# A block's finer steps on another table of openings, and its leftovers run at the block's close

## The chip, the core and the metric

One program runs on one core of a Trainium2 chip. The metric is the device time in microseconds (us). The engines are TensorE (PE in the profile), VectorE (DVE), ScalarE (ACT), GpSimd (POOL) and the queue of SyncE (SP), which only issues DMAs here.

## The reference, cut to what matters

`x` has 16 graphs of 1024 nodes with 128 features, and all share one sparse adjacency matrix (about 8 edges a node). Four layers follow one another: attention, graph attention, attention, attention.

```python
# attention layer (L0, L2, L3): 8 heads of 16
Q, K, V = h @ Wq, h @ Wk, h @ Wv
scores = einsum('bnhd,bmhd->bhnm', Q, K) / sqrt(16)          # -inf where adj == 0
attn_out = einsum('bhnm,bmhd->bnhd', softmax(scores), V)
x = layer_norm(h + attn_out @ Wo + bo, ln1)
x = layer_norm(x + relu(x @ W1 + b1) @ W2 + b2, ln2)
# graph attention layer (L1): one head
h = x @ W
e = leaky_relu(h @ a_src + (h @ a_dst).T, 0.2)                # -inf where adj == 0
x = layer_norm(softmax(e) @ h + x)
```

## The kernel before, in words

The kernel works on the edges alone. Nodes are sorted by degree into eight tiles of 128 (t = 0 to 7); the 16 graphs form two groups of eight (g = 0, 1), and a group two halves of four. A unit is a layer, a group and a tile, (l, g, t); there are 64 of them, in this order. I call the stretch in which the edges of one unit are worked on its block.

A block has parts: pairs of gathered slots, and one part with a single mixed slot, which is always part 3. Tile 0 has six parts, tiles 1 to 6 have five, tile 7 has four. So the block of tile 0 is the long one, that of tile 7 the short one. In an attention layer DVE does three operations on every part i, at 2.3 us each (1.2 us for the mixed one): the product of gathered keys and queries (`products`, L963), the reduction to scores (L986), and, one part later, the weighting of the gathered values with the exponentials (`weighted`, L1014). The exponential is made by ACT (L990). The keys and values come by indirect DMA, issued by POOL (L951) four parts ahead into one of four buffers; a buffer is free again after the weighting. The products have four buffers of their own. PE gives one back when `summed` (L1030, `acc<-pr,marks`) has added a part up. Parts 0 and 1 are added up together, at the start of the third iteration.

When all parts of a unit are added up, PE sums the denominators (`divided`, L1030 `ps<-ex,marks`), and DVE divides (L1067, L1070). The division stands in DVE's queue behind the first weighting of the next block. What follows is the unit's tail: output projection, two layer norms, the hidden layer, and the projection to the next layer's table. It runs on PE and ACT, beside the next block. There are two tails, a for half 0 and b for half 1. Each is a generator with these steps:

- 1: transposes of o on PE (L647), copy on ACT (L653). 2: bias, ACT (L716). 3: Wo and centring, PE (L720, L721).
- 4: squares, ACT (L624). 5: Ln and Exp, ACT (L630, L631). 6: scaling, ACT (L640).
- 7: transposes of z on PE (L647), gain and shift on ACT (L655). 8 and 9: the two halves of W1 on PE (L731) with the ReLU on ACT (L740).
- 10 and 11: W2 and centring, PE (L745, L749). 12 to 14: as 4 to 6. 15: transposes and gain for the new state (L647, L655); from here on the tail counts as free.
- 16 and 17: projection to the next layer (PE L576, ACT L580; to the graph layer L596). 18: the table is written by SP. In the last layer 16 transposes back, and 18 writes the output by POOL; there no tail ever counts as free, so it always runs to its end.

A third kind of generator stands in the list `fronts`: the queries of the next unit (`queries`). Its steps for half 0 are: Wq on PE (L904) and a copy to q (L908); four replications on PE (L913) and two copies to qr (L916); the other two copies. The same three follow for half 1; the seventh call finds it at its end. In the first group of layer 0 the list also holds `slots`, which makes index tiles: PE spreads (L413) and DVE unpacks (L427). After the fronts come `loads` (state of a later unit; in layer 0 with transposes of x, L647) and `slow` (the first projection of the second group, in layer 0 alone).

The order is written out by hand: the engines work through their queues as the program puts the instructions there. Between DVE's operations the main loop calls `others()`, which I call an opening. After the division of an attention unit the openings are counted from 0, and each takes one string from the table `PLAN`: "a" and "b" run one step of tail a or b, "q" one step of the fronts. The openings fall as follows in a block of five parts, D being the division:

- entry 0 follows D. 1, 2, 3 follow product 2, its reduction, and the weighting of part 1.
- 4, 5, 6 follow product 3 (mixed), its reduction, and the weighting of part 2. The sum of parts 0 and 1 is put into PE's queue just ahead of entry 4.
- 7, 8, 9 follow product 4, its reduction, and the weighting of part 3.
- 10, 11, 12 follow product 0 of the next block, its reduction, and the weighting of part 4. 13 and 14 follow product 1 of that block and its reduction; the denominators are put ahead of 13. Then comes the next D.

So a block of five parts has 15 openings, that of six 18 and that of four 12. Past the end of the table an opening runs "abq". Where an attention unit is to be closed and a tail isn't yet free, the loop in lines 1243 to 1247 runs further openings until both are. What a tail has not done by then it does in the next block, ahead of the new tail of its half, since `planned` steps the first generator it finds.

Of the kernel before, what the change touches and what calls it, by code (L numbers as in the profile page):

```python
# [137 lines left out]
def sparse_path(ctx: ExitStack, tc: tile.TileContext, a: dict, out: bass.AP, flag):  # L138
# [64 lines left out]
    def gather_buffer():  # L203
        return gathers.tile([P, max(4 * ROW, J * (ROW + G))], F32, tag="e", name="e")
# [605 lines left out]
    def at_once(g):  # L810

        spare = reps.tile([P, J, ROW], F32, tag="qr", name="spare")

        def fetch(t):
            if t < T:
                nc.sync.dma_start(
                    spare[:, t % J, :], a["x"][t * P : (t + 1) * P, columns(g, 0, HF)]
                )

        for t in range(3):  # L820
            fetch(t)
        yield
        for t in range(T):
            fetch(t + 3)
            rows = spare[:, t % J, :].rearrange("p (h g d) -> p h g d", h=HF, g=GH)
            both = []
            for h in range(HF):
                kv = None
                if h:
                    kv = (hidden, queries_of_shared)[t % 2]()  # L830
                    kv = kv.rearrange("p (c g d) -> p c g d", c=2, d=D)
                both.append(natural(g, t, h, rows[:, h], kv))
            while both:
                advance(both)
                yield

    PLAN = (
        "qaaqqbaba", "", "aq", "abb", "a", "qaba", "abbqabba", "", "baqbaba", "qqb", "bqaa", "", "b", "qbqqqbq", "ba",
    )

    def exponents():
# [14 lines left out]
    def is_attention(u):  # L856
        return LAYERS[units[u][0]][1] is ATTN
# [101 lines left out]
    def products(i):  # L959
        u, (piece,) = parts[i]  # L960
        n = len(piece)
        prs[i] = [prods.tile([P, 2, ROW], F32, tag="pr", name="pr")]
        nc.vector.tensor_tensor(  # L963
            prs[i][0][:, :n, :], es[i][:, :n, :ROW],
            qx[u].rearrange("p (o c) -> p o c", o=1) if (MIX, 0) in piece
            else of_piece(qs[u], piece),
            ALU.mult,
        )
# [132 lines left out]
    opening = [None]  # L1101
    half_of = {}

    def step(gen, gens):
        got = next(gen, "end")
        if got == "end":
            gens.remove(gen)
        elif got == "free":
            free.append(gen)

    def planned(beyond="abq"):
        n = opening[0]
        opening[0] += 1
        for c in PLAN[n] if n < len(PLAN) else beyond:
            if c == "q":
                aside()
                continue
            for gen in tails:
                if half_of[gen] == "ab".index(c):
                    step(gen, tails)  # L1120
                    break
# [18 lines left out]
    def aside():  # L1140
        while True:
            gens = fronts or loads or idle()
            if not gens:
                break
            got = next(gens[0], "end")
            if got == "end":
                gens.pop(0)
                continue
            if got == "idle":
                advance(idle())  # L1150
            break
# [3 lines left out]
    with tc.manual_schedule():  # L1155
        wide = [gather_buffer() for _ in range(EDGES)]
        setup, entry, weights = graph(wide), at_once(0), load_weights("L0")
        next(setup)
        next(weights)
        next(entry)  # L1160
        more = [weights, load_graph_weights()]
        rest = slots()
        for i, room in enumerate(setup):
            if i == T:
                for gen in more:
                    next(gen)
            if room == "load":
                for _ in loaded(0):
                    next(entry, None)
            elif room == "queries":  # L1170
                for _ in entry:
                    pass
                for _ in queries(0):
                    pass
            elif isinstance(room, str):
                next(rest)
            else:
                for _ in range(room):
                    next(entry, None)
        for _ in entry:  # L1180
            pass
        scratch.close()
        prods = ctx.enter_context(tc.tile_pool(name="prods", bufs=4))
        smalls = ctx.enter_context(tc.tile_pool(name="smalls", bufs=3))
        slow.append(at_leisure(1))
        second = loaded(1)
        next(second)
        for i in range(AHEAD - 1):
            gathered(i)
        nc.gpsimd.memset(wide[3], 0.0)  # L1190
        gathered(AHEAD - 1)
        fronts.extend([islice(rest, 4), second] + more)
        closing, sizes = None, ()
        begun = 0
        for i in range(len(parts) + 2):
            here = i < len(parts)
            u = parts[i][0] if here else len(units)
            if here:
                l = units[u][0]
                eager[0] = 1 if u < 2 else 0  # L1200
                if i and parts[i - 1][0] != u:
                    begun = i
                    if u < T - 1:
                        fronts.append(islice(rest, 4))
                    if l + 1 < len(LAYERS) and LAYERS[l + 1][1] is ATTN:
                        if units[u][1:] == (0, 1):
                            more = load_weights(LAYERS[l + 1][0])
                            next(more)
                            next(more)
                        if units[u][1:] == (0, 4):  # L1210
                            fronts.append(more)
                if is_attention(u):
                    products(i)
            if i > 1:
                summed(i - 2)
                done = parts[i - 2][0]
                if parts[i - 1 : i] == [] or parts[i - 1][0] != done:
                    closing = divided(done)
                    next(closing)
            others()  # L1220
            if here:
                exponentials(i)
            if here and i == begun + 1:
                if is_attention(u):
                    shared(u)
                while loads:
                    advance(loads)
                if u + 1 < len(units):
                    fronts.append(queries(u + 1))
                loads.append(loaded(u + 2))  # L1230
                if u:
                    advance(loads)
            others()
            if 0 < i <= len(parts):
                weighted(i - 1, 0)
                if not is_attention(parts[i - 1][0]):
                    others()
                    weighted(i - 1, 2)
                gathered(i - 1 + AHEAD)
                for _ in sizes:  # L1240
                    pass
            if closing is not None and here:
                while any(gen not in free for gen in tails):
                    if opening[0] is None:
                        advance(tails)
                    else:
                        planned("ab")
                next(closing)
                sizes, closing = closing, None
                passes = 3 if is_attention(u) else 4  # L1250
                steps = STEPS if is_attention(done) else GRAPH_STEPS
                steps -= LATE[units[done][0]]
                pace[:] = 0.0, steps / (passes * sum(part[0] == u for part in parts) - 1)
                if is_attention(done) and opening[0] is None:
                    for gen in list(tails):
                        if gen in free:
                            for _ in gen:
                                pass
                            tails.remove(gen)
                opening[0] = 0 if is_attention(done) else None  # L1260
            others()
            if i + 1 >= len(parts) or parts[i + 1][0] != u:

                while fronts:
                    advance(fronts)
        while opening[0] < len(PLAN):
            planned()
        while tails:
            advance(tails)
        for _ in closing:  # L1270
            pass
        while tails:
            advance(tails)
# [435 lines left out]
```

## Time and profile before

| | |
|---|---|
| median of 3 runs | 2240.71 us (2234.82 to 2246.4) |
| the profiled execution | 2224.11 us |
| its span on the core | 2222.3 us, clock granted to TensorE 0.958 on the mean |
| steady blocks (tiles 1 to 6), division to division | 33 to 36 us; in layer 0, group 0, about 42.8 us |
| blocks around a short one, e.g. from 1289.3 us | 32.8 us (short), then 45.1 us (long) |

A row of the groups or of a timeline gives the line, the engine, the operation and the tiles (out<-in); in a timeline the start and the duration come first, and brackets at the end hold the idle time of the engine before the row and what ended it. A line of the waits says which engine and line waited for which, how long in total, how often, and the longest.

### The profile page before, as it was taken

The page shows a single profiled execution, that of the slowest core. Times are in us where ns is not written, and L with a number is a line of the kernel's source. Part 1 is how long each engine was busy: PE and PEld are TensorE (multiplying, and loading weights), DVE is VectorE, ACT ScalarE, POOL GpSimd, SP SyncE. Part 2 cuts the span into 40 slices and gives each one's busy share as a digit, 9 for nine tenths or more (in the row PEclk, how much of TensorE's full clock was granted, in tenths as well). Part 3 has the DMA queues.
Part 4 walks back from the last instruction along what each step waited for, and adds up shares of the span by engine and source line. Part 5 has one row for each costly group of instructions (what it writes and reads, how often), then busy time and mean ns, then how long its engine had stood idle before and what let it go on. Part 6 is the DMA issues. An engine that isn't in the chain of part 4 may idle for free.

```text
span 2222.3 us, 36516 instructions
## 1 busy us (share of the span) xinstructions
PE 2009.0 (90%) x13140; PEld 1265.3 (57%) x13140; DVE 1874.3 (84%) x1472; ACT 1520.1 (68%) x5041; POOL 1029.4 (46%) x699
## 2 busy tenths in 40 slices
PE   7589998989999889989899998999989899989986
PEld 5446665655665555555466665656655555555654
DVE  7887888889998477767999988999888988899892
ACT  3337776868887555556587886888767777677774
POOL 3342433444455477774444535355343444454540
PEclk8799999999999999999999999999999999999998
DMA  7888777768988699998888987899878788678850
GB/s 257 292 298 279 285 248 269 281 235 298 323 318 295 209 332 354 351 348 320 319 320 323 330 292 277 314 335 326 291 270 303 272 284 283 224 278 298 285 210 21
DMA packets 164701, 636.05 MB, mean 286 GB/s; under 512 B 34569, under 2 KB 37385, under 8 KB 116015
## 3 DMA queue, kind: packets, MB, share of 16 engines
q0 software_dynamic: 88720, 485.08, 61.1%
q1 hardware_dynamic: 75792, 148.57, 19.4%
q8 instruction: 105, 1.72, 0.3%
q14 instruction: 84, 0.68, 0.1%
HBM read 581.08 MB, written 92.34 MB: 303 GB/s over the span
## 4 chain that ended last, share of the span: by engine, by line
PE 57%; DVE 14%; ACT 12%; issue 9%; DMA 5%; POOL 3%; POOLq 0%; DVEq 0%; ACTq 0%
PE acc L1030 14%; PE ps L647 6%; PE ps L913 6%; PE yps L745 6%; PE ps L576 5%; PE ps L731 5%; DMA e<-table,idx 4%; DVE pr L1014 4%; PE yps L721 3%; PE yps L720 3%; DVE pr L963 3%; PE yps L749 3%; DVE sc L986 2%; ACT f L740 2%; POOL e L951 2%
## 5 line engine op out<-in xcount | busy, mean ns | idle before, releaser
L951 POOL DMA_INDIRECT e<-table,idx x576 | 882.2, 1532 | 1017.7 <-DVE pr L1014 750.9
L1014 DVE TENSOR_TENSOR pr<-e,ex 128x2048 f32<-128x2048 f32 (+1 forms) x320 | 661.5, 2076 | 59.5 <-ACT ex L990 31.9
L963 DVE TENSOR_TENSOR pr<-e,qr 128x2048 f32<-128x2048 f32 x192 | 443.4, 2309 | 116.4 <-ACT qr L916 71.3
L1030 PE MATMUL acc<-pr,marks 128*32 128x512 f32 x2624 | 506.5, 608 | 30.7 <-DVE o L1070 19.1
L986 DVE TENSOR_REDUCE sc<-pr 128x128 f32<-128x2048 f32 (+1 forms) x240 | 497.5, 2073 | 8.0
L624 ACT ACTIVATE z<-yps,root 128x128 f32<-128x128 f32 x888 | 315.4, 377 | 71.3 <-PE yps L749 36.2
L745 PE MATMUL yps<-W,f 128*128 128x128 f32 x1520 | 253.2, 284 | 19.1 <-ACT f L740 19.1
L1030 PEld LDWEIGHTS acc<-pr,marks 128*32 128x32 f32 x2624 | 107.6, 110 | 285.0 <-issue 230.8
L745 PEld LDWEIGHTS yps<-W,f 128*128 128x128 f32 x1520 | 203.2, 191 | 99.4 <-ACT f L740 61.1
L640 ACT ACTIVATE z<-yps,rstd 128x128 f32<-128x128 f32 x888 | 253.8, 373 | 3.0
L916 ACT COPY qr<-ps 128x512 f32<-128x512 f32 x384 | 202.4, 595 | 30.4 <-PE ps L913 24.2
L580 ACT COPY kv<-ps 128x512 f32<-128x512 f32 x176 | 103.3, 593 | 173.2 <-PE ps L576 162.6
L576 PE MATMUL ps<-Wkv,xT 128*128 128x256 f32 x768 | 205.2, 409 | 15.2 <-ACT xT L653 13.1
L731 PE MATMUL ps<-x,W 128*128 128x512 f32 x384 | 187.5, 611 | 15.7 <-ACT x L655 15.7
L913 PE MATMUL ps<-q,rep 32*128 32x512 f32 x768 | 186.4, 688 | 13.4 <-ACT q L908 11.9
L624 ACT ACTIVATION_READ_ACCUMULATOR z<-yps,root 128x1 f32 x888 | 191.7, 216 | 0.0
L576 PEld LDWEIGHTS ps<-Wkv,xT 128*128 128x128 f32 x768 | 144.9, 201 | 69.0 <-ACT xT L653 16.8
L740 ACT ACTIVATE f<-ps,b 128x512 f32<-128x512 f32 x190 | 129.9, 684 | 77.9 <-PE ps L731 77.3
L647 PE MATMUL ps<-ident,z 128*128 128x128 f32 x896 | 152.4, 286 | 14.0 <-ACT z L640 10.9
L721 PE MATMUL yps<-centre,x 128*128 128x128 f32 x768 | 158.4, 290 | 2.7 <-ACT x L716 2.3
L720 PE MATMUL yps<-Wo,oT 128*128 128x128 f32 x768 | 159.6, 292 | 0.6 <-ACT oT L653 0.4
L647 PEld LDWEIGHTS ps<-ident,z 128*128 128x128 f32 x896 | 106.1, 141 | 77.0 <-ACT z L640 49.6
(176 smaller groups left out, 2594.8 us busy)
## 6 DMA issues: line engine op xcount, KB each, us to landing
table<-kv SPq DMA_DIRECT2D x88, 512.0 KB, 7.1
kept<-xT SPq DMA_DIRECT2D x96, 256.0 KB, 5.3
x<-kept SPq DMA_DIRECT2D x48, 512.0 KB, 9.0
qx<-qr SPq DMA_DIRECT2D x48, 256.0 KB, 7.3
e<-table,idx POOLq DMA_INDIRECT x576, 8.0
table<-kv SPq DMA_DIRECT2D x32, 256.0 KB, 8.6
qx<-qr SPq DMA_DIRECT2D x18, 384.0 KB, 6.5
qx<-qr SPq DMA_DIRECT2D x42, 128.0 KB, 5.2
```

The lines of the kernel that those rows point to most:

```text
L576: nc.tensor.matmul(ps[:, k, :], x[:, i + k, :], w[LAYERS[l][0], "Wkv"], start=True, stop=True,)
L624: nc.scalar.activation(z[:, i, :], y[:, i, :], AF.Square, scale=D**-0.5, bias=root, accum_out=total[:, i : i + 1],)
L640: nc.scalar.activation(z[:, i, :], y[:, i, :], AF.Copy, scale=rstd[:, i : i + 1])
L647: nc.tensor.transpose(ps[:, i, :], z[:, i, :], ident)
L731: nc.tensor.matmul(ps, p["W1"][:, f * P : (f + 1) * P], x1.rearrange("p g n -> p (g n)"), start=True, stop=True,)
L745: nc.tensor.matmul(ps[:, i, :], f1[:, f, i * P : (i + 1) * P], p["W2"][:, f, :], start=(f == 0), stop=False,)
L913: nc.tensor.matmul(ps, rep_of(j), q[32 * j : 32 * j + 32], start=True, stop=True)
L951: nc.gpsimd.indirect_dma_start(out=es[i][:, k, :], out_offset=None, in_=tables[l, g][:, :], in_offset=bass.IndirectOffsetOnAxis(ap=idx[:, ...
L963: nc.vector.tensor_tensor(prs[i][0][:, :n, :], es[i][:, :n, :ROW], qx[u].rearrange("p (o c) -> p o c", o=1) if (MIX, 0) in piece else of_p ...
L986: nc.vector.tensor_reduce(sc[:, :n, :], prs[i][0][:, :n, :].rearrange("p k (a d) -> p k a d", d=HD), mybir.AxisListType.X, ALU.add,)
L1014: nc.vector.tensor_tensor(prs[i][k0 // 2][:, :m, :].rearrange("p k (a d) -> p k a d", d=d), es[i][:, k0 : k0 + m, base : base + ROW].rearr ...
L1030: nc.tensor.matmul(outs[32 * j : 32 * j + 32], marks[:, mark, :], rhss, start=(chunk == mine[0]), stop=(chunk == mine[-1]),)
```

## The change

The table `PLAN` holds the same numbers of steps (18 a, 18 b, 15 q over its 15 entries) in other places. And where a unit is closed, all entries of the table that are left are run, after both tails are free and ahead of the division.

```diff
     PLAN = (
-        "qaaqqbaba", "", "aq", "abb", "a", "qaba", "abbqabba", "", "baqbaba", "qqb", "bqaa", "", "b", "qbqqqbq", "ba",
+        "qaaqqba", "baqba", "aq", "a", "bbaa", "abq", "baqbbaa", "", "aqbbba", "", "bbqaa", "b", "", "qqqqbbqq", "ba",
     )
...
                         advance(tails)
                     else:
                         planned("ab")
+                while opening[0] is not None and opening[0] < len(PLAN):
+                    planned()
                 next(closing)
```

By the step numbers above, counted through the two tables, the steps stand in these entries (steps that stay are left out; the calls of q are counted from the queries' first in entry 0):

| step | before | after |
|---|---|---|
| b2, a4 | 0 | 1 |
| a5, query 4 (Wq of half 1) | 2 | 1 |
| b3 | 3 | 1 |
| a6 | 3 | 2 |
| query 5 (replications of half 1, two copies) | 5 | 2 |
| a7 | 4 | 3 |
| b4 | 3 | 4 |
| b5, a8, a9 | 5 | 4 |
| a10, b6 and query 6 (the last two copies) | 6 | 5 |
| a13 | 8 | 6 |
| b13 | 9 | 10 |
| b15 | 12 | 11 |
| query 7 (their end) | 8 | 6 |
| the two calls of q after it | 9, 9 | 8, 13 |

In PE's queue of a steady block two groups change places: the four L913 of half 1 and tail a's four L647 `ps<-ident,z` stood behind the eight L1030 that add up parts 0 and 1, and now stand ahead of them. In layer 0, group 0, four L647 `ps<-ident,x` move from ahead of the spread L413 to behind the denominators. On ACT the last two copies to qr stood behind tail b's L655 and now stand ahead of it. In the short blocks' successors the queries, b's projection and step 18 of both tails come ahead of the new tails' first transposes.

## The prediction

> **What bounds the kernel now.** I read the page's busy times, then single blocks by stretch, the waits, then timelines of single blocks. No engine is full over the span, and none can be named from these shares alone.
>
> ```profile
> PE 2009.0 (90%) x13140; PEld 1265.3 (57%) x13140; DVE 1874.3 (84%) x1472; ACT 1520.1 (68%) x5041; POOL 1029.4 (46%) x699
> ```
>
> The busy time by stretch, for single blocks (columns: length, then busy us of PE, PE's weight loads, DVE, ACT and POOL, clock, DMA share, GB/s), shows where the limit is. The first row is a block of layer 0, group 0; the second one of layer 0, group 1; then a short block, the long one after it, and two neighbours of layer 3.
>
> ```profile
> 298.60:341.30 42.70, 38.77 (x248) 25.88 (x248) 35.70 (x39) 29.70 (x101) 16.11 (x11) 0.92 0.74 261
> 566.20:599.60 33.40, 32.55 (x230) 20.84 (x229) 32.42 (x19) 27.96 (x99) 16.95 (x11) 1.00 0.92 330
> ...
> 1289.30:1322.10 32.80, 31.76 (x216) 21.30 (x214) 25.48 (x17) 27.64 (x88) 11.11 (x8) 1.00 0.79 278
> 1322.10:1367.20 45.10, 39.58 (x229) 22.39 (x230) 39.16 (x23) 28.38 (x89) 20.22 (x13) 1.00 0.77 264
> 1978.40:2013.60 35.20, 33.28 (x213) 20.44 (x214) 32.19 (x19) 25.76 (x85) 17.34 (x11) 0.90 0.85 304
> 2013.60:2048.60 35.00, 32.25 (x220) 19.68 (x218) 32.38 (x19) 27.09 (x88) 18.93 (x12) 1.00 0.80 292
> ```
>
> A steady block holds 32.3 us of DVE work and lasts 33 to 36 us: DVE sets the pace, PE is nearly as full, and only what makes DVE wait can be won. So the waits of DVE, by line (total, times, longest):
>
> ```profile
> DVE pr L963 <- ACT qr L916: 71.3, 22, 8.4
> ...
> DVE pr L1014 <- ACT ex L990: 31.9, 19, 5.3
> ...
> DVE pr L963 <- DMA e<-table,idx: 28.7, 23, 2.6
> ...
> DVE little L427 <- PE ps L413: 16.2, 5, 3.4
> DVE pr L963 <- PE acc L1030: 8.5, 10, 3.7
> ```
>
> The largest is the first product of a block (product 0), waiting for the last copy of its queries: 22 times, it starts just as that copy ends. The timeline of DVE in the block whose division is at D = 1978.40 shows this and a second, hidden limit.
>
> ```profile
> 1978.40 0.55 DVE L1067 RECIPROCAL both<-ps 128x64 f32<-128x64 f32 x1
> ...
> 1991.77 2.32 DVE L963 TENSOR_TENSOR pr<-e,qr 128x2048 f32<-128x2048 f32 x1
> ...
> 2000.20 2.29 DVE L963 TENSOR_TENSOR pr<-e,qr 128x2048 f32<-128x2048 f32 x1 [2.65 <-ACT qr L916]
> ```
>
> PE between the same times:
>
> ```profile
> 1989.81 1.92 PE L1030 MATMUL acc<-pr,marks 128*32 128x512 f32 x16
> 1991.67 0.66 PE L647 MATMUL ps<-ident,z 128*128 128x128 f32 x4
> 1992.25 2.06 PE L913 MATMUL ps<-q,rep 32*128 32x512 f32 x8
> 1994.24 1.98 PE L731 MATMUL ps<-x,W 128*128 128x512 f32 x4
> ```
>
> The product at 1991.77 (product 4) takes the buffer that this sum (L1030, ahead of entry 4) gives back. It starts 0.04 us after the sum ends: in this block it is late by 0.1 us already. Call the sum's end S, counted from D. Over the blocks S is 13.4 to 14.0 in layer 0 group 0 and where layer 3 was throttled, 11.1 to 11.3 in layer 0 group 1, 10.8 to 11.9 in layer 2; product 4 could start at 13.2. So the sum has 1.3 to 2.4 us to spare in unthrottled blocks and none in the others.
>
> **What the Trainium skill says.** "PSUM — Partial Sum Buffer", section "Engine vs sequencer instructions": ScalarE and VectorE queues are strictly first in, first out, and matmuls run in program order. The trace agrees: the transposes and the queries' matmuls follow the sum without a gap, in the program's order. So whatever is put ahead of the sum delays it by its full length. "TensorE: Matmul & The Clock Gate", section "What's actually happening": half clock after an idle window of some 3.4 us. The trace agrees roughly: idle of 2.85 to 3.8 us before the first transposes after D is followed by 6.8 us at clock 0.5 in five blocks of layer 0 and every other one of layer 3; idle of 1.67 us (at 1321.9) was not.
>
> **The change part by part.** DVE's order, POOL's and its gathers stay; steps on PE and ACT move, and with them their SP writes (table L585 and L610, state L568, 5 to 9 us to landing). Those I cost at nothing: the gathers that read them belong to the next layer, a whole group of eight blocks later.
>
> *1. Queries and step a7 move ahead of the sum.* Old: the four replications of half 1 (L913) in entry 5, a's transposes (step 7) in entry 4, both after the sum. New: entries 2 and 3, both ahead of it. From the second timeline their length is 1992.25 − 1991.67 = 0.58 plus 1994.24 − 1992.25 = 1.99 = 2.58 us. Their inputs are there in time (the q copy moves up behind the squares), so the sum ends at S + 2.58, and product 4 starts at S + 2.62 where that is over 13.2. From product 4 to product 0 DVE needs 5.99 us (13.14 to 19.13 in layer 0 group 1, without a wait): product 0 not before S + 8.61.
> In return the last query copies no longer stand behind b's step 7: on ACT they follow the two ReLUs and the scaling. From the L731 matmuls to the second ReLU's end 2.76, the exponential 0.2, scaling 1.05, copies to release 0.6: queries at S + 2.5 + 4.6 = S + 7.1. Old: S + 8.46 (13.33 + 8.46 = 21.79 = 2000.20 − 1978.40; 11.09 + 8.46 = 19.55, seen 19.55).
> So in a steady block the old wait for queries is taken over by a wait for the sum: S + 8.46 becomes S + 8.61. In 18 steady blocks bound by queries that is 18 × 0.15 = **+2.7 us**. In the others product 0 waits for its gather, whose issue hangs on a weighting ahead of product 4: a gain or loss of nothing, covered by that transfer.
>
> *2. Short blocks* (tile 7: four parts, product 0 of the next block comes right after entry 6; waits 6.5, 7.1, 7.1, 6.0 us). Here no product 4 lies between, so the queries at S + 7.1 instead of S + 8.46 count: 4 × 1.36 = **−5.4 us**.
>
> *3. Layer 0, group 0.* A transposition of x (L647, 0.55 us) moves from entry 9 past the spread (L413), for which DVE waits 3.4 us in five blocks: 5 × 0.55 = **−2.8 us**.
>
> *4. Entries left over.* After a short block in layers 0 and 2 (and at 2→3), the old code leaves b three steps and a one step behind; the long block then ends with waits of 4.33 + 2.31, 4.92 + 0.71 and as much again: 17.9 us. The new loop runs b's projection (steps 16, 17) and the queries at once, ahead of the first transposes. The trace shows this only in layer 3, where the old loop already ran all (division at 1897.7): 5.28 us wait at L1014, at half clock. At full clock I count on ACT, ahead of o's transposes, 2.05 + 0.5 + 1.2 + 2.05 of copies, then to the exponential: it ends at D + 13.3 instead of 10.9, 2.3 us late, and the sum costs another 1.3: 3.65 per block. Ends: 3 × 3.65 − 17.9 = −6.9; with half clock 3 × 6.95 − 17.9 = +3. I take **−5**.
> *5.* Layer 3's own long block: +0.5 (exponential behind step 5; the sum +1.7, of which a later 1.17 wait is saved). Blocks after long ones: waits of 0.8 to 1.2 us from the lag shrink, 3 × −0.5. The first block of layers 0 and 2 loses 0.6 each. Together **+0.2**. Graph layer: only leftovers move, nothing.
>
> Sum: 2.7 − 5.4 − 2.8 − 5 + 0.2 = −10.3 us on the profiled execution's own 2224.11 us (span 2222.3 and 1.8 around it). The median of the runs shown, 2240.71, is 16.6 above that execution; the same share, −0.46%, gives 2230.4, rounded to **2230**.
>
> **Rivals.**
> *R1, the clock recovers.* PE idle before D is 2.85 us in group 0; with the 0.55 us moved into it and DVE earlier by 0.4 it is 1.9. If half clock then stays away in five blocks and in some of layer 3, S falls by 2.6 and product 0 with it: up to 10 × 2.5 more, 2205 to 2225. Against it: idle of 2.1 (at 383.6) still throttled.
> *R2, the boundary pays nothing.* The three long blocks behave like layer 3's: 8 us of my gain go, 2238, no change.
> *R3, slower: the sum's wait comes on top.* Product 4 is late by 2.58 less the slack, 0.2 to 1.3 us in some 40 unthrottled or gather-bound blocks. If the weighting behind it, and so the gathers that it releases, then come late by as much, and each lost time is not given back at product 0, a block loses 0.5 to 1.2: +20 to +48 on my 2230, that is 2250 to 2278. It decides from 0.5 us per block (0.26 eats my gain). For it: the two DMA queues together are busy 80% of the span. Against: the weighting that frees product 0's buffer lies ahead of product 4.
> *R4, nothing but a permutation:* in layer 3 the new loop has nothing to run; then only part 1 to 3 count, 2235.
>
> **How the numbers follow.** A measurement here can tell about 0.5% (11 us) from no change. Forecast 0.50 (half of it over 0.5%), R1 0.16, R2 and R4 0.18, R3 0.16 (0.02 of it within 0.5%). Faster 0.25 + 0.16 = 0.41; slower 0.14; same 0.25 + 0.18 + 0.02 = 0.45. The range leaves out the farther half of R1 and of R3: 2208 to 2256; the forecast's own is 2222 to 2238.
>
> **What would show it.** L963 ← ACT qr falls from 71 to some 25 us (short blocks and the layer starts are left); L963 ← PE acc rises from 8.5 to over 25. In steady blocks S is 2.5 later, product 0 within 0.3 us of its old place. In short blocks the wait is 4.7 to 5.8. Long blocks wait early (D + 13), not at D + 35. A block length of layer 2 changed by over 0.5 us, or another clock pattern, would make this wrong.

## The result, and the profile after

| | before | after |
|---|---|---|
| median, 19 runs each in turn | 2231.42 us | 2219.80 us |
| ratio of after to before | | 0.9939, 95% interval 0.9917 to 0.9962 |
| the profiled execution | 2224.11 us | 2221.51 us |
| its span and mean clock | 2222.3 us, 0.958 | 2219.3 us, 0.955 |

The change gains 0.61%; 0.46% was forecast. The time named, 2230 us, was that share taken off the three runs shown, whose median was 2240.71; 19 runs put the kernel before at 2231.42, and 2219.80 lies 2 us below the forecast's own 2222 to 2238. So it is the share that was met. The busy times of the page hardly move, as an exchange of places should have it:

```profile
PE 1993.9 (90%) x13140; PEld 1260.8 (57%) x13140; DVE 1873.2 (84%) x1472; ACT 1525.9 (69%) x5041; POOL 1028.0 (46%) x699
```

Busy time by stretch, for single blocks of after (columns as in the prediction): layer 0 group 0, layer 0 group 1, a short block, the long one after it, two neighbours of layer 3.

```profile
299.90:341.65 41.75, 37.29 (x248) 25.20 (x248) 36.10 (x40) 30.00 (x101) 16.50 (x11) 0.92 0.75 261
565.30:598.20 32.90, 31.82 (x231) 20.68 (x230) 32.45 (x20) 28.16 (x100) 17.85 (x11) 1.00 0.94 336
1290.60:1321.20 30.60, 29.15 (x204) 19.48 (x203) 25.48 (x17) 26.14 (x85) 11.11 (x8) 1.00 0.84 304
1321.20:1367.80 46.60, 43.75 (x245) 24.92 (x244) 39.13 (x23) 31.01 (x94) 18.40 (x13) 1.00 0.74 257
1973.60:2009.60 36.00, 33.52 (x214) 21.24 (x215) 32.23 (x20) 25.94 (x85) 13.78 (x10) 0.87 0.83 293
2009.60:2045.80 36.20, 31.29 (x219) 19.29 (x217) 32.26 (x19) 27.19 (x88) 16.58 (x12) 0.99 0.84 297
```

The short block is 2.2 us shorter than in the prediction's fence, the long one 1.5 us longer, with 4 us more of PE's work in it. Layer 3 still changes between full and reduced clock from block to block. Now the waits of DVE in after:

```profile
DVE pr L1014 <- ACT ex L990: 47.1, 33, 8.4
DVE pr L963 <- PE acc L1030: 40.6, 27, 4.8
...
DVE pr L963 <- DMA e<-table,idx: 22.1, 19, 3.6
DVE pr L963 <- PE ps L647: 18.9, 5, 5.0
...
DVE little L427 <- PE ps L413: 13.1, 5, 3.3
...
DVE pr L963 <- ACT qr L916: 12.1, 2, 6.8
```

The wait for the queries, the largest before with 71.3 us, is down to 12.1. The 18.9 us put down to L647 belong with it: 17.9 of them are the short blocks, where product 0 still starts just as the last copy to qr ends (the record of that copy ends 0.46 us after the product's start, as it did before). In its place stands the wait for the sum, 40.6 us after 8.5. The block with its division at 1973.56 shows the exchange, first on DVE, then on PE:

```profile
1973.56 0.55 DVE L1067 RECIPROCAL both<-ps 128x64 f32<-128x64 f32 x1
...
1990.31 2.29 DVE L963 TENSOR_TENSOR pr<-e,qr 128x2048 f32<-128x2048 f32 x1 [2.15 <-PE acc L1030]
...
1995.97 2.28 DVE L963 TENSOR_TENSOR pr<-e,qr 128x2048 f32<-128x2048 f32 x1
```

```profile
1985.97 1.14 PE L913 MATMUL ps<-q,rep 32*128 32x512 f32 x8
1987.76 0.66 PE L647 MATMUL ps<-ident,z 128*128 128x128 f32 x4 [0.66 <-ACT qr L916]
1988.35 1.92 PE L1030 MATMUL acc<-pr,marks 128*32 128x512 f32 x16
```

Replications and transposes now run ahead of the sum. Product 4 waits 2.15 us for it, at D + 16.7, and product 0 comes at D + 22.4 without a wait. In the prediction's block it came at D + 21.8 with a wait of 2.65.

One profile is not enough for a difference of 14 us, and the first profile of before lay under its median. A second one was taken of each kernel (runs `before_again` and `after_again`). These are the lengths of blocks, from division to division, added up by kind, in us:

| kind (blocks) | before, two profiles | after, two profiles | only the table | only the loop | loop without queries |
|---|---|---|---|---|---|
| layer 0 group 0, its first block | 48.5, 49.1 | 53.8, 52.3 | 52.3 | 49.0 | 52.1 |
| layer 0 group 0, next five | 206.9, 206.9 | 203.7, 201.9 | 201.6 | 205.9 | 198.7 |
| short (4) | 129.3, 128.9 | 120.3, 121.9 | 121.2 | 129.9 | 121.9 |
| long after short (4) | 182.0, 181.9 | 186.5, 184.2 | 186.2 | 183.7 | 173.8 |
| first after a long one (3) | 103.5, 103.4 | 101.3, 101.4 | 103.0 | 101.6 | 101.9 |
| other steady ones of layers 0 (group 1) and 2 (15) | 509.3, 508.6 | 509.4, 506.2 | 507.6 | 512.1 | 505.9 |
| graph layer (16) | 317.2, 318.6 | 318.3, 317.2 | 326.4 | 317.3 | 316.9 |
| steady ones of layer 3 (12) | 425.8, 426.3 | 430.3, 429.6 | 421.8 | 425.1 | 423.4 |

### The profile page after: what moved, and what is told of

Its sections match the earlier page's. It is cut to its first block, busy times and chain, and to the rows that moved or that the text cites. A ratio compares the mean times of both kernels' runs of the same rounds, so it can differ in the third digit from the quotient of the medians.

```text
span 2219.3 us, 36551 instructions
## 1 busy us (share of the span) xinstructions
PE 1993.9 (90%) x13140; PEld 1260.8 (57%) x13140; DVE 1873.2 (84%) x1472; ACT 1525.9 (69%) x5041; POOL 1028.0 (46%) x699
## 4 chain that ended last, share of the span: by engine, by line
PE 58%; DVE 13%; issue 12%; ACT 8%; DMA 5%; POOL 3%; POOLq 0%; DVEq 0%; ACTq 0%
PE acc L1030 14%; PE ps L647 6%; PE ps L731 6%; PE yps L745 6%; PE ps L913 5%; PE ps L576 5%; DMA e<-table,idx 4%; DVE pr L1014 4%; PE yps L721 3%; PE yps L720 3%; POOL e L951 3%; PE yps L749 3%; DVE pr L963 3%; PE ps L904 2%; DVE sc L986 2%
## 5 line engine op out<-in xcount | busy, mean ns | idle before, releaser
L1014 DVE TENSOR_TENSOR pr<-e,ex 128x2048 f32<-128x2048 f32 (+1 forms) x320 | 661.6, 2076 | 76.1 <-ACT ex L990 47.1
L1030 PE MATMUL acc<-pr,marks 128*32 128x512 f32 x2624 | 505.8, 608 | 27.7 <-DVE o L1070 12.9
L963 DVE TENSOR_TENSOR pr<-e,qr 128x2048 f32<-128x2048 f32 x192 | 440.1, 2292 | 100.3 <-PE acc L1030 40.6
L1030 PEld LDWEIGHTS acc<-pr,marks 128*32 128x32 f32 x2624 | 106.7, 110 | 285.2 <-issue 241.6
L745 PE MATMUL yps<-W,f 128*128 128x128 f32 x1520 | 253.2, 284 | 16.7 <-ACT f L740 16.3
L647 PE MATMUL ps<-ident,z 128*128 128x128 f32 x896 | 154.3, 286 | 39.1 <-ACT qr L916 19.0
L624 ACT ACTIVATION_READ_ACCUMULATOR z<-yps,root 128x1 f32 x888 | 185.3, 209 | 0.0
L913 PE MATMUL ps<-q,rep 32*128 32x512 f32 x768 | 164.8, 698 | 16.8 <-ACT q L908 10.5
L647 PEld LDWEIGHTS ps<-ident,z 128*128 128x128 f32 x896 | 107.5, 142 | 90.3 <-ACT qr L916 43.0
```

The lines of the kernel that those rows point to most:

```text
L624: nc.scalar.activation(z[:, i, :], y[:, i, :], AF.Square, scale=D**-0.5, bias=root, accum_out=total[:, i : i + 1],)
L647: nc.tensor.transpose(ps[:, i, :], z[:, i, :], ident)
L745: nc.tensor.matmul(ps[:, i, :], f1[:, f, i * P : (i + 1) * P], p["W2"][:, f, :], start=(f == 0), stop=False,)
L913: nc.tensor.matmul(ps, rep_of(j), q[32 * j : 32 * j + 32], start=True, stop=True)
L963: nc.vector.tensor_tensor(prs[i][0][:, :n, :], es[i][:, :n, :ROW], qx[u].rearrange("p (o c) -> p o c", o=1) if (MIX, 0) in piece else of_p ...
L1014: nc.vector.tensor_tensor(prs[i][k0 // 2][:, :m, :].rearrange("p k (a d) -> p k a d", d=d), es[i][:, k0 : k0 + m, base : base + ROW].rearr ...
```

## The experiments

A ratio is to runs of the kernel before on the same chip, in turn. The medians of before there were 2231.1 us for `table_only`, `loop_only`, `after_again` and `loop_no_queries`, 2228.0 for `before_again`, `query_behind_sum`, `mixed_in_place` and `filler`, and 2221.7 for the other four.

**The two halves alone.** `table_only` has the new table without the loop.

```diff
-                while opening[0] is not None and opening[0] < len(PLAN):
-                    planned()
```

> Only the new table; the leftovers' loop at the close is taken out. Theory T (the table pays in the four short blocks, about 2.2 us each, and is level in the steady ones; the loop costs in the long blocks): the short blocks stay at about 30 us, the long ones go back to about 45.5, and the time is some 4 us below the changed kernel, 0.992 of the kernel before. Rival L (the loop's early run is itself the gain, as the prediction's part 4 had it, 9.9 us over short and long blocks together): the time is 5 us above the changed kernel, 0.996. The wait of products for the sum (L963 <- PE acc) stays at about 40 us under both.

Measured: 2224.81 us, 0.9987 (0.9969 to 1.0006).

`loop_only` has the loop with the old table.

```diff
-        "qaaqqba", "baqba", "aq", "a", "bbaa", "abq", "baqbbaa", ...
+        "qaaqqbaba", "", "aq", "abb", "a", "qaba", "abbqabba", ...
```

> Only the leftovers' loop, on the old table. Theory T: the short blocks keep their old 32 us (product 0 there still waits 6 to 7 us for the queries), the long ones get the clump of queries and b's projection ahead of the transposes of o and cost about 1 us each more than before: +4 us, 1.002 of the kernel before. Rival L: -5 us, 0.998. L963 <- ACT qr stays at about 70 us.

Measured: 2223.56 us, 0.9972 (0.9957 to 0.9987).

`after_again` is the changed kernel.

> The changed kernel itself, for a second profile and a comparison on the same chip: 0.994 of the kernel before; L963 <- PE acc about 40 us, L1014 <- ACT ex about 47.

Measured: 2213.96 us, 0.9931 (0.9906 to 0.9956).

Theory T falls, and rival L, the prediction's own part 4, stands: the loop is worth 0.28% alone, the table 0.13% (its interval includes no change), together 0.69%; within the intervals they add up. T had been read off the first two profiles, in which the long blocks grew. The table of blocks shows what was overlooked: they grow by as much with the new table alone, 186.2 us. What the loop changes beside that table is the graph layer, 326.4 us without it, in the one profile of `table_only`, and 317 to 318 with it. The surplus is in three of its blocks: those of tiles 0 and 1 in group 0 take 62.7 us together (before 56.5 and 57.2, with the loop 52.3), that of tile 0 in group 1 takes 29.3 (before 21.5, with the loop 24.0 to 27.8); other blocks give part of it back.

`before_again` is the kernel before.

> The kernel before itself, for a second profile of it. The first one (2224.1 us) lies 7 us under the median of 35 runs (2231.1). If the four short blocks are again 31.6 to 32.8 us and the steady ones of layer 3 are longer than in the first profile, the first was a lucky one and the difference of the first two profiles (3 us) says less than that of the medians.

Measured: 2222.49 us, its short blocks 31.6 to 32.8. So the block table compares profiles of before that lie 5 to 7 us under the medians of their chips with profiles of after that lie 1 to 2 us above theirs; that of `loop_only` lies 4 us above. From the first division to the last the profiles account for 5.6 us of the gain; which blocks hold the rest is not shown.

**The clump of queries.** At the close of a short block the loop runs the queries' steps in a row; I call that the clump. `loop_no_queries` keeps the loop, but not its calls of q: `planned` then skips the letter q of a string.

```diff
-                    planned()
+                    planned(queries=False)
```

> The changed kernel, but the leftovers' loop skips the calls of q, so that the queries keep to the openings of the long block; b's projection and the tables' writes are still run at the close. Theory C (the queries in the clump are the larger part of what delays the exponential): the transposes of o move from D + 10.5 to about D + 5, the wait at the first L1014 of a long block falls from 5.5 to below 2, each of four long blocks is 3 to 5 us shorter, 12 to 20 us in all: 0.986 to 0.989 of the kernel before. Rival P (b's projection is what counts, or the queries only move the wait to the next product 0): less than 1.5 us a block, 0.992 to 0.994.

Measured: 2203.26 us, 0.9888 (0.986 to 0.9917): theory C. The long block of after, with D = 1321.2, first on DVE, then what ACT does ahead of the copies of o (L653):

```profile
1337.77 2.29 DVE L1014 TENSOR_TENSOR pr<-e,ex 128x2048 f32<-128x2048 f32 x1 [5.53 <-ACT ex L990]
1341.04 2.29 DVE L963 TENSOR_TENSOR pr<-e,qr 128x2048 f32<-128x2048 f32 x1 [0.98 <-PE acc L1030]
```

```profile
1322.58 0.58 ACT L908 COPY q<-ps 128x512 f32<-128x512 f32 x1
1324.37 1.56 ACT L916 COPY qr<-ps 128x512 f32<-128x512 f32 x3 [1.21 <-PE ps L913]
1326.17 0.58 ACT L916 COPY qr<-ps 128x512 f32<-128x512 f32 x1 [0.23 <-PE ps L913]
1327.31 0.59 ACT L908 COPY q<-ps 128x512 f32<-128x512 f32 x1 [0.56 <-PE ps L904]
1328.12 0.58 ACT L580 COPY kv<-ps 128x512 f32<-128x512 f32 x1 [0.22 <-PE ps L576]
1328.99 0.59 ACT L580 COPY kv<-ps 128x512 f32<-128x512 f32 x1 [0.28 <-PE ps L576]
1330.04 1.56 ACT L916 COPY qr<-ps 128x512 f32<-128x512 f32 x3 [0.47 <-PE ps L913]
1331.83 0.59 ACT L916 COPY qr<-ps 128x512 f32<-128x512 f32 x1 [0.23 <-PE ps L913]
1332.31 0.22 ACT L1080 COPY both<-ps 128x64 f32<-128x64 f32 x1
1332.42 0.60 ACT L653 COPY oT<-ps 128x512 f32<-128x512 f32 x1
```

From 1322.58 to 1332.31 ACT copies 6.6 us and waits for PE 3.2 us (the brackets added). PE, between the same times, waits for ACT:

```profile
1323.22 1.13 PE L913 MATMUL ps<-q,rep 32*128 32x512 f32 x6 [0.70 <-ACT q L908]
1325.01 1.12 PE L913 MATMUL ps<-q,rep 32*128 32x512 f32 x2 [0.66 <-ACT qr L916]
```

Each engine waits for the other by turns, since a replication needs the copy of q and a copy needs the replication. Without the queries in the clump the waits in the same long block (1309.62 to 1352.68 in that kernel) are:

```profile
DVE pr L963 <- PE acc L1030: 2.1, 1, 2.1
DVE pr L1014 <- ACT rstd L630: 0.9, 1, 0.9
DVE both L1067 <- PE ps L1030: 0.4, 1, 0.4
DVE pr L1014 <- ACT ex L990: 0.2, 1, 0.2
```

3.6 us instead of 7.1, and the block lasts 43.1 us instead of 46.6. The four long blocks together lose 11.5 us (173.8 after 185.4 on the mean); the two kernels' medians differ by 10.7. Other rows of that one profile moved too, by up to 6.6 us, but the long blocks did the same again below: 190.4 us in `mixed_in_place`, and 177.6 and 173.5 in `all_three` and `all_four`, which leave these calls out.

**Is the sum's wait the price?** `query_behind_sum` puts query 5 back behind the sum, into entry 4.

```diff
-        "aq", "a", "bbaa", "abq",
+        "a", "a", "qbbaa", "abq",
```

> The changed kernel with query 5 (four replications, two copies) back behind the sum, first in entry 4; step a7 stays ahead of it. Theory S: the sum ends 2 us earlier (L963 <- PE acc 39 -> about 12, L3 unthrottled S 13.2 -> 11.3), the queries at the same place as now, so product 0 comes 0.6 us earlier in throttled blocks and no earlier elsewhere: 6 to 7 us, 0.990 to 0.991 of the kernel before. Rival G: 0.993 to 0.994. If the last copies then stand behind tail b's steps again, L963 <- ACT qr comes back with over 30 us and the time is that of the kernel before.

Measured: 2241.66 us, 1.0062 (1.0039 to 1.0085), slower than both kernels. The wait for the sum fell to 18.3 us, but that for the exponential (L1014 <- ACT ex L990) rose to 91.0 us, 81 times. The block with its division at 575.0, first on ACT, then on DVE:

```profile
588.22 1.07 ACT L916 COPY qr<-ps 128x512 f32<-128x512 f32 x2 [2.12 <-PE ps L913]
...
592.22 0.25 ACT L990 ACTIVATE ex<-sc 128x64 f32<-128x64 f32 x1
...
599.76 0.29 ACT L990 ACTIVATE ex<-sc 128x128 f32<-128x128 f32 x1
```

```profile
592.95 1.22 DVE L1014 TENSOR_TENSOR pr<-e,ex 128x1024 f32<-128x1024 f32 x1
...
600.09 2.29 DVE L1014 TENSOR_TENSOR pr<-e,ex 128x2048 f32<-128x2048 f32 x1 [1.40 <-ACT ex L990]
```

Entry 4 lies ahead of the mixed part's exponential (592.22) in ACT's queue. The copies waited there for replications that now stood behind the sum, and what follows on ACT came late. In this block the mixed part's weighting (592.95) was not held up by it, but that of part 4 was. Over the blocks of tiles 2 to 6 in the three attention layers the weighting of part 4 waits 32.0 us, 25 times (in after 2.1 us, 4 times), and that of the mixed part 10.0 us, 16 times (in after never). Neither theory had this. So the same step was tried one opening later, behind that exponential, as `query_in_entry_5`:

```diff
-        "aq", "a", "bbaa", "abq",
+        "a", "a", "bbaa", "qabq",
```

> The changed kernel with query 5 first in entry 5, where it is behind both the sum and the exponential of the mixed part (query_behind_sum had put it ahead of that exponential, which then waited 2.1 us behind the copies for PE). Only step a7 delays the sum now: S 2 us earlier than in the changed kernel, 11.3 and not 13.2 at full clock. The last copies come about as far behind the changed kernel's sum as now (S + 1.98 + 2.06 for PE, then copies, scaling and copies: 4.3 us behind where the sum ended). Theory S: L963 <- PE acc falls from 39 to about 12 us, L1014 <- ACT ex stays near 45, throttled blocks gain 1 to 2 us: 10 to 20 us in all, 0.984 to 0.989 of the kernel before. Rival Q (the queries' later place on ACT eats it): 0.993 or more.

Measured: 2211.54 us, 0.9952 (0.9932 to 0.9972): rival Q, with no gain over after. L963 <- PE acc is 17.0 us, but L963 <- ACT qr is back at 34.3 and L1014 <- ACT ex at 60.2. In the same blocks the mixed part's weighting never waits now, that of part 4 still 14.3 us, 10 times. What one wait gives up the others take.

**A product buffer more.** `mixed_in_place` takes the sum out of product 4's way without moving a step.

```diff
-        prs[i] = [prods.tile([P, 2, ROW], F32, tag="pr", name="pr")]
+        prs[i] = [
+            qx[u].rearrange("p (o c) -> p o c", o=1) if (MIX, 0) in piece
+            else prods.tile([P, 2, ROW], F32, tag="pr", name="pr")
+        ]
```

> The changed kernel, but the product of the mixed part is written over qx instead of into a product buffer. A block then needs four product buffers for its other parts, and product 4 has a free one without the sum of parts 0 and 1. Theory S (the wait for the queries was exchanged for one for the sum): L963 <- PE acc falls from 39 to under 10 us; product 0 is then held by the queries, 4.6 us behind the sum, or by its gather, so throttled steady blocks (S 16.3) gain 0.9 us and the others nothing, the long ones 1 us: 10 to 14 us in all, 0.987 to 0.989 of the kernel before. Rival G (gathers hold the blocks anyway): the wait vanishes but L963 <- DMA and the exponential's waits take over, under 3 us, 0.992 to 0.994.

Measured: 2182.75 us, 0.9802 (0.9768 to 0.9836), 29 us below the changed kernel by the ratios and twice what theory S allowed. But the twelve steady blocks of layer 3 alone gain those 29 us, 400.8 after 430, and the rest balances; the fifteen of layers 0 and 2 went from 506 or 509 to 504.7, and in layer 0, group 0, five blocks took 201.9, as before the edit. The wait for the sum is gone, as theory S had it, but it was not what counted. The same edit on the old table decides it, `mixed_in_place_old`:

> The kernel before with the same single edit as mixed_in_place (the mixed part's product over qx). There L963 <- PE acc is 9 us, against 39 in the changed kernel. Theory S (the edit is worth 30 us in the changed kernel because the new table had put the sum in DVE's way): here product 0 stays bound by the queries at S + 8.46, L963 <- ACT qr stays near 70 us, and 2 to 7 us are won, 0.997 to 0.999 of the kernel before. Rival B (a fifth buffer's worth of room is a gain by itself, under any table, as for instance by ending the change of full and half clock in layer 3): 20 us or more, below 0.991.

Measured: 2189.58 us, 0.9869 (0.9849 to 0.9889). Rival B: theory S falls for this edit. Layer 3's blocks take 398.7 us here. Its steady blocks of group 0 by stretch, before, then with the edit:

```profile
1650.30:1866.10 215.80, 198.31 (x1290) 122.68 (x1290) 193.81 (x109) 158.59 (x516) 90.74 (x65) 0.94 0.81 287
```

```profile
1644.50:1843.80 199.30, 189.09 (x1290) 115.19 (x1290) 194.04 (x108) 157.72 (x516) 114.11 (x65) 1.00 0.87 305
```

DVE's work is the same, 194 us, the clock is whole, and DVE is busy 97% of the time. The waits for gathers in these stretches (L963 <- DMA) fell from 10.5 to 1.5 us, and those for queries (L963 <- ACT qr), 8.0 us before, are no longer among them. What I take to have set this off is in SyncE's queue (start, time in the queue). Before, in the block with D = 1685.9:

```profile
1702.18 6.70 SPq L927 DMA_DIRECT2D qx<-qr  x2
1708.98 0.53 SPq L879 DMA_DIRECT2D x<-kept  x1
```

With the edit, in the same block, D = 1678.3:

```profile
1706.40 1.14 SPq L927 DMA_DIRECT2D qx<-qr  x2
1707.59 0.97 SPq L879 DMA_DIRECT2D x<-kept  x1
```

The load of qx moved from D + 16 and D + 22 to D + 28, and with it the 512 KB of x, since qx is now in use until the mixed part is summed. Before, both ran while the gathers for products 0 and 1 were under way; where all landings are recorded (two parts in each group), those for product 1 took, from the first issue to the last landing, 15.3 and 13.7 us on the mean in the two groups of layer 3, and 12.0 and 11.3 in `mixed_in_place`. In layer 0, group 1, and layer 2 most loads of qx stood at D + 32 to D + 34 already, in both kernels; the writes of tables and states stand ahead of them there, which layer 3 doesn't have. There the edit gains nothing. I read it so: late gathers stretch a block, PE idles ahead of the next division, the clock is halved, and the next block's queries come late. The edit gives every attention layer the buffer and moves the loads in layer 3 alone, and of these layers' steady blocks only those of layer 3 gain; that speaks for the loads. That the transfers' time is the first link is not shown alone: no run moved them and nothing else.

**What a whole clock is worth.** `filler` gives PE idle work ahead of the division.

```diff
+                if units[done][:2] in ((0, 0), (3, 0), (3, 1)) and units[done][2] < T - 2:
+                    spare = bank([P, 512])
+                    for _ in range(3 if units[done][0] else 2):
+                        nc.tensor.matmul(
+                            spare, ident, rep.rearrange("p j s n -> p (j s n)")[:, :512],
+                            start=True, stop=True,
+                        )
                 next(closing)
```

> The changed kernel with idle work on PE: ahead of the division of steady blocks, where PE idles 3 to 4 us, two (layer 0, group 0) or three (layer 3) more matmuls 128x512 whose result nobody reads, 1.0 us each by the row of L731. It asks what rival R1 (the clock recovers) would have been worth. If the idle time is what makes the half clock, the granted clock rises from 0.957 to over 0.975 and S in layer 0 group 0 falls from 15.9 to 13.2. Theory R1: product 0 follows, 2 us a block in 10 blocks, 0.984 to 0.986 of the kernel before. Rival G (in layer 3 every other block is full clock already and no shorter, since its gathers come late): only layer 0 gains, 8 to 12 us, 0.988 to 0.990. Should PE, with 2 to 3 us more work, become the limit: 0.994 or more.

Measured: 2198.05 us, 0.9871 (0.9833 to 0.9909), mean clock 0.972 in the profile. A block of layer 0 group 0 and one of layer 3:

```profile
342.57:381.63 39.06, 36.60 (x252) 24.17 (x252) 35.69 (x38) 29.91 (x101) 17.77 (x11) 1.00 0.81 282
1702.06:1737.67 35.61, 34.08 (x222) 20.46 (x221) 32.30 (x19) 27.18 (x88) 16.18 (x12) 1.00 0.81 287
```

The clock is whole in both. The five blocks of layer 0 take 191.0 us instead of 202 to 204, 2.4 us less each, as R1 priced it (2.5); layer 3's twelve take 416 instead of 430. So the time lies between the two forecasts: layer 3 gained too, which rival G had left out, and the mean clock of the runs, 0.969, stayed under the 0.975 named. A whole clock alone leaves layer 3 at 34.7 us a block on the mean, where the edit of the mixed part reaches 33.2 to 33.4.

**Both gains together.** `all_three` is the changed kernel with the edit of the mixed part and the loop without queries; `all_four` adds the filler in layer 0, group 0.

> The changed kernel with both edits that gained: the mixed part's product over qx, and a leftovers' loop without the calls of q. If they are independent their gains add up: 30 + 11 us below the changed kernel, 0.975 of the kernel before; if both work by the same waits, no better than mixed_in_place, 0.980.

Measured: 2161.54 us, 0.973 (0.9709 to 0.9751). They add up.

> The same with the idle matmuls of filler, in layer 0, group 0 alone (in layer 3 mixed_in_place runs at full clock in all but two of 14 blocks without them). Added up: another 9 to 12 us, 0.970 of the kernel before; none if product 0 of these blocks is then held by gathers or queries.

Measured: 2155.20 us, 0.9711 (0.9692 to 0.973). The five blocks of layer 0 fell by 10.7 us in the profile, but the step from `all_three` is within the two intervals. This is the fastest version of all, 2.3% below the changed kernel if the two ratios are divided.

## Why the prediction was right, point by point

The share came near in part by luck, since terms that failed offset one another: in the profiles the short blocks gained 8.0 us for the 5.4 forecast, the first block of layer 0 lost 4 for 0.6, and the long blocks lost 3.4 where some 5 were to be gained. And the profiles place only 5.6 us of the gain.

**Part 1, the exchange, was right.** At full clock in layer 3 the sum ends at D + 13.18, after 10.80: 2.38 us later, and 2.5 on the mean where the clock is reduced, priced 2.58. The wait for queries went from 71 to 12 or, with the short blocks, 30 us (forecast 25), that for the sum from 8.5 to 40.6 (forecast over 25). Blocks of layers 0 (group 1) and 2 kept their length to 0.1 us on the mean; those of layer 3 are 0.3 us longer (priced 0.15). Two figures of the sum were off: the waits for queries lie in 16 steady blocks and not 18, and from product 4 to product 0 DVE needs 5.66 us (1990.31 to 1995.97 above); in the 5.99 a product of 2.54 us is contained, where most take 2.28. `query_in_entry_5` went half the way back and gained nothing: these waits take each other's place.

**Part 2, the short blocks, was too small.** Waits of 4.40, 4.95, 4.28 and 4.28 us in the first profile, of 4.41, 5.40, 5.40 and 4.29 in the second, forecast 4.7 to 5.8; a block gains 2.0 us, not 1.36. The terms that failed are the sum's shift, which is 1.9 and 2.4 us there and not 2.5, and product 0's distance from the sum, 4.3 and not 4.6.

**Part 3, layer 0 group 0, was right in its term:** L427's wait fell by 3.1 us (forecast 2.8). But the first block of the group lost 4 us, forecast 0.6: its sum ends at D + 23.6 and 22.1 in the two profiles instead of 18.2. There the early projections of the second group stand ahead of the sum too, and PE waits 3.5 and 3.3 us for ACT over the block, 0.7 and 0.4 before. I had counted matmuls there and not the waits between them.

**Part 4 met its number, but not by its mechanism.** The loop alone gains 0.28%, 6 us (forecast 5), but not where the gain was forecast: in the profile of `loop_only` short and long blocks together take 313.6 us, before 311.3 and 310.8, and no row of its column shows where the 6 us are. That the number fits is luck. The late wait of the long blocks went, as forecast; the early one that takes its place measures 6.5 us at full clock and not 3.65, since the exponential ends at D + 16.5 and not 13.3. The term counted ACT's copies and left out the 3.2 us of turns between PE and ACT. In after, short and long blocks together gained 4.6 us instead of 9.9. "Graph layer: only leftovers move, nothing" was wrong beside the new table: there the loop takes back some 9 us, by the one profile of `table_only`.

**Part 5:** three blocks after long ones gain 2.1 us together, forecast 1.5.

**The rivals.** R1 didn't come: clock 0.955 and 0.958 in the profiles of after, 0.958 and 0.956 in those of before; `filler` shows that its price was right. The prediction's reading of the clock was too narrow: in before half clock also followed idle times of 2.05, 2.65 and 4.91 us in layer 3, and lasted 3.4 or 10.2 us in some blocks; the 1.67 us that were not followed by it there (at 1321.9) were in `mixed_in_place_old` (1.67 us ahead of 1315.6). R2 came by half: the long blocks do behave like layer 3's, but the short ones gave 2.6 us more than forecast, and the loop paid elsewhere. R3 didn't come: the sum's wait is there 27 times, and the 15 blocks of layers 0 and 2 have not grown by it. R4 falls with `loop_only`, whose interval (0.9957 to 0.9987) lies below 1.

## What to carry to other kernels

When work is put ahead of a result that others wait for, count not only its instructions but the turns between the engines that it contains, and ask for each queue what it now blocks: one opening too early cost 1.1% here. Waits that take each other's place are worth nothing one at a time; the gains lay in what set them off, a clump at the close and, as I read it, loads that ran beside the gathers. Two profiles misled about the halves of a 14 us change where timed runs of each half did not.

## What the runs showed of the hardware

Over all single executions the mean granted clock and the time go together: within one kernel the correlation is -0.79, and 0.001 of clock goes with 1.8 us (before: 0.952 to 0.962 in its runs). More than half of the scatter thus goes with how often PE was slowed. And 2 or 3 us of matmuls whose result nobody reads, put ahead of the division, keep the clock whole: of 17 divisions so prepared, half clock followed one in `filler` and 11 in after, where PE had been idle for 2.8 to 4.9 us. "TensorE: Matmul & The Clock Gate" of the Trainium skill, section "What's actually happening", states that the clock falls to half after an idle window of about 3.4 us, and so leads one to expect this; here idle times from 2.05 us on were followed by half clock in before. That filling them pays 0.6% (0.9871 after 0.9931; the two intervals just touch) in a kernel whose PE is already 90% busy, I had not expected.
